# One gate product over two PSUM banks for a pair of channels, in a fused convolution block

## The chip, the cores and the metric

The kernel runs on one core of a Trainium2 chip. The metric is the device time of one execution in microseconds (us); the median of several executions is compared. PE is the matmul engine (PEld its weight loads, which overlap the matmuls), DVE the vector engine, ACT the scalar (activation) engine, POOL and SP issue DMAs. SBUF is the working memory, PSUM the memory in which matmuls add up, in eight banks of 512 fp32 values for each of 128 partitions.

## The reference

The input is 16 images of 192 channels and 64 x 64 pixels, in fp32. Two layers follow each other; the change lies in the first, between the two projections:

```python
h = layernorm_over_channels(x)
pg = conv1x1(h, in_proj_w, in_proj_b)             # 192 -> 384 channels
projected, gate = split(pg, 2, axis=1)
projected = dwconv3(projected, dw_k)              # 3x3, every channel by itself
scanned = directional_scan(projected, ...)        # s = d*s + (1-d)*cur, from left, right, top, bottom, mixed
local = dwconv3(projected, le_k)
mixed = (scanned + local) * sigmoid(gate)
bn = batchnorm(mixed)                             # mean and variance over images and pixels
x = x + conv1x1(gelu(bn), out_proj_w, out_proj_b)
x = x + fc2(gelu(fc1(layernorm_over_channels(x))))
```

The second layer multiplies every image with a 3 x 3 kernel of four taps that it computes from the image's means.

## The kernel before, in words

Three stages follow each other. The first (to about 640 us) normalizes, projects to 384 channels and writes the result to DRAM. The second (about 650 to 1326 us) does the convolutions, the scans, the gate and the statistics of the batch norm. The third (to the end) does everything else, per chunk of 512 pixels. The order of instructions on each engine is written out by hand: the instructions stand on every engine in the order in which the program issues them, and an engine waits at the head of its queue.

In the second stage the 192 channels are worked on in 24 groups of eight (GC = 8), and each group in four pairs (hp_ = 4) of channels c and c + 4, so that the loop runs over 96 pairs k. Partitions hold the columns of images (64 of one half of the 16 images, 64 of the other); a channel has 512 values per partition. The tile `pg` of a group holds all projected values (index 0) and gate values (index 1) of its eight channels, in 32 blocks of 16 values per channel, and there are three buffers of it (low, pg_o, mid). Per pair:

- `depthwise(k)` (L618): 40 matmuls over columns of `pg` into the PSUM tile `ps_d` (two banks, two buffers); ACT evacuates them to `q` (L631, L633).
- `tables(k)`, `scans(k)`: ACT writes two decay tables (L641), DVE runs a scan over all 1024 values forwards (L653) and one backwards (L655) into `v`.
- `local(k)` and `vertical(k)` (L662): 24 matmuls of `q` and then 16 of `v`, all adding into `ps_l`. Channel c adds into one bank and c + 4 into another. Each bank is a tile of its own, from four buffers.
- `sigmoid(k)` (L683): ACT writes the sigmoids of the two gate channels to two tiles `sg`, of which there are two buffers in all.
- `gate(k)`: for each of the two channels DVE multiplies the bank by the sigmoids (L696, 512 values) into the channel's place in `pg`, from which `bn_stats` (L697) takes the moments of that channel.

One round of the loop issues, in this order: tables of pair k+1; vertical and gate of pair k-1; scans of k+1; depthwise of k+2; local and sigmoid of k. So DVE's queue holds gate(k-1), scans(k+1), gate(k), and so on; PE's vertical(k-1), depthwise(k+2), local(k); ACT's tables(k+1), the evacuation of depthwise(k+2), sigmoid(k).

At the end of a group POOL stores its products to DRAM (L707), and SP loads the group three later into the same buffer (L605) once that store has landed. The matrices of the depthwise (dm, L190) and of the local and vertical matmuls (lm, L197) are loaded per group too, half on SP and half on POOL. `spread` and `batch_norm` turn the moments of the first 128 channels into scale and bias in rounds 76 and 77, with small matmuls (L723, L735) into tiles from the buffers of `ps_l`, and those of the last 64 after the loop; `hidden_bias` uses such a buffer before the loop. The third stage starts behind the last of these.

Of the kernel before, what the change touches and what calls it, by code (L numbers as in the profile page):

```python
# [21 lines left out]
F32 = mybir.dt.float32  # L22
# [9 lines left out]
CH = 512  # L32
# [8 lines left out]
GC = 8  # L41
NCG = C // GC
BR = 16
NB = HW // BR
# [11 lines left out]
def conv_block_kernel(ctx: ExitStack, tc: tile.TileContext, x, prm, w_in, w_out, w_fc1, b_fc1, w_fc2, w1, bn1, w2, out):  # L56
    nc = tc.nc
# [79 lines left out]
    def hidden_bias(pb):  # L137
        for m in range(NFC):
            for t in range(3):
                nc.tensor.matmul(pb[:, m:m + 1], wf1[0:64, t, 128 * m:128 * m + 128],  # L140
                                 pt3[0:64, t, LN2B:LN2B + 1], start=(t == 0), stop=(t == 2))
        nc.vector.tensor_add(bf1, bf1, pb[:, 0:NFC])
# [25 lines left out]
    stats = ce.tile([128, C, 6], F32, tag="stats", name="stats")  # L168
# [12 lines left out]
    lm_of = lambda g: lm_first if g == 1 else mats[g % 2]["lm"]  # L181
# [4 lines left out]
    def load_dm(g):  # L186
        for i, q in enumerate(HALF):
            v = dv_d[g, :, 0:1, :]
            src = bass.AP(v.tensor, v.offset, [[GC, HW], [128 * GC, 3], [1, HW * GC]])
            (nc.sync, nc.gpsimd)[i].dma_start(mats[g % 2]["dm"][q].rearrange("p k m c -> p k (m c)"), src)  # L190
# [396 lines left out]
    with ExitStack() as stage:  # L587
# [3 lines left out]
        wb = stage.enter_context(tc.tile_pool(name="wb", bufs=2))  # L591
        psb = stage.enter_context(tc.tile_pool(name="psb", bufs=2, space=PSUM))

        n_bp = C // 2
        hp_ = GC // 2
        grp = [dict() for _ in range(NCG)]
        bst = [dict() for _ in range(n_bp)]
# [38 lines left out]
        def tables(k):  # L636

            bst[k]["tab"] = []
            for d in range(2):
                tab = wb.tile([128, 2 * CH], F32, tag=f"tab{d}", name=f"tab{d}")  # L640
                nc.scalar.activation(tab.rearrange("p (n h) -> p n h", h=HW), mask[:, d].broadcast_to([128, n_img_all, HW]),  # L641
                                     AF.Copy, scale=dec_b[:, d, k:k + 1])
                bst[k]["tab"].append(tab)
# [14 lines left out]
        def lmul(k, m, src, dst, start, stop):  # L658
            g, c = divmod(k, hp_)
            for i, q in enumerate(HALF):  # L660
                for ih, o in enumerate(HALF):
                    nc.tensor.matmul(dst(bst[k]["ps"][i][o]), lm_of(g)[q, m, :, c], src(q, ih), start=start, stop=stop)  # L662

        def local(k):
            bst[k]["ps"] = [psb.tile([128, CH], F32, tag="l", name="ps_l", bufs=4) for _ in range(2)]
            img = lambda a: a.rearrange("p (n h) -> p n h", h=HW)
            q = bst[k]["q"]
            lmul(k, 1, lambda h, ih: q[h, ih], lambda a: a, True, False)
            lmul(k, 0, lambda h, ih: img(q[h, ih])[:, :, 0:HW - 1], lambda a: img(a)[:, :, 1:HW], False, False)
            lmul(k, 2, lambda h, ih: img(q[h, ih])[:, :, 1:HW], lambda a: img(a)[:, :, 0:HW - 1], False, False)  # L670

        def vertical(k):
            for d in range(2):
                lmul(k, 3 + d, lambda h, ih: bst[k]["v"][d][h, ih], lambda a: a, False, d == 1)

        def sigmoid(k):
            g, c = divmod(k, hp_)
            bst[k]["sg"] = []
            for i in range(2):
                ch = c + hp_ * i  # L680
                n = g * GC + ch
                sg = wb.tile([128, CH], F32, tag="sg", name="sg", bufs=2)
                nc.scalar.activation(sg.rearrange("p (i j b) -> p i j b", b=NB, j=BR),  # L683
                                     grp[g]["pg"][:, :, 1, ch].rearrange("p (i b) j -> p i j b", b=NB),
                                     AF.Sigmoid, bias=bias_g[:, n:n + 1])
                bst[k]["sg"].append(sg)

        def gate(k):
            g, c = divmod(k, hp_)
            s = grp[g]  # L690
            blocks = lambda a: a.rearrange("p (n j) -> p n j", j=BR)
            for i in range(2):
                ch = c + hp_ * i

                o = s["pg"][:, :, 0, ch]
                nc.vector.tensor_mul(o, blocks(bst[k]["ps"][i]), blocks(bst[k]["sg"][i]))  # L696
                nc.vector.bn_stats(stats[:, g * GC + ch], o)  # L697
            bst[k].clear()
            if c == hp_ - 1:
                if g == NCG - 1:  # L700

                    for i in range(2):
                        for wh in range(2):
                            w0_ = 32 * wh
                            (nc.sync, nc.gpsimd)[wh].dma_start(y_low[2 * w0_ + 32:2 * w0_ + 64, 2, i, LASTC * BR:],
                                                              s["pg"][w0_:w0_ + 32, i * NB, 0].rearrange("p c j -> p (c j)"))
                nc.gpsimd.dma_start(mixed_d[:, :, :, g].rearrange("i b p e -> p (i b) e"),  # L707
                                    s["pg"][:, :, 0].rearrange("p n c j -> p n (c j)"))
                s.clear()


        def moments(cls):
            chs = (slice(0, 128), slice(128, C))[cls]

            v = stats.rearrange("p c (e k) -> p k e c", k=3)
            return v[:, 1, :, chs], v[:, 2, :, chs], dev[:, :, chs]

        def spread(cls):
            means, sums2, dv = moments(cls)
            n = (128, C - 128)[cls]  # L720
            pm = psb.tile([128, CH], F32, tag="l", name="pm", bufs=4)
            for e in range(2):
                nc.tensor.matmul(pm[:, 0:n], ones, means[:, e], start=(e == 0), stop=(e == 1))  # L723
            nc.vector.scalar_tensor_tensor(dv, pm[:, 0:n].unsqueeze(1).broadcast_to([128, 2, n]), -1.0 / 256.0, means,
                                           ALU.mult, ALU.add)
            nc.vector.tensor_mul(dv, dv, dv)
            nc.vector.scalar_tensor_tensor(dv, sums2, 2.0 / (n_half * HW), dv, ALU.mult, ALU.add)

        def batch_norm(cls):
            means, _, dv = moments(cls)  # L730
            pq = psb.tile([128, CH], F32, tag="l", name="pq", bufs=4)
            for part in (slice(0, 128),) if cls == 0 else HALF:
                for j, src in enumerate((means, dv)):
                    for e in range(2):
                        nc.tensor.matmul(pq[part, j:j + 1], src[:, e], ones[:, 0:1], start=(e == 0), stop=(e == 1))  # L735
            nc.vector.tensor_scalar_mul(mv[:, cls], pq[:, 0:2], 1.0 / 256.0)
            sc, bi = bn_sc[:, cls:cls + 1], bn_bi[:, cls:cls + 1]
            nc.scalar.activation(sc, mv[:, cls, 1:2], AF.Sqrt, bias=eps5)
            nc.vector.reciprocal(sc, sc)
            nc.vector.tensor_mul(sc, sc, pv[:, cls, BNW:BNW + 1])  # L740
            nc.vector.tensor_mul(bi, sc, mv[:, cls, 0:1])
            nc.vector.tensor_sub(bi, pv[:, cls, BNB:BNB + 1], bi)
# [8 lines left out]
        for k in range(-2, n_bp + 1):  # L751
            if 0 <= k + 1 < n_bp:
                tables(k + 1)
            if k >= 1:
                vertical(k - 1)
                gate(k - 1)
                g, c = divmod(k, hp_)
                if c == 0 and 0 < g < NCG - 1:
                    load_lm(g + 1)
                if c == 0 and g == 3:  # L760
                    load_weights(2)
                if c == 0 and g + 2 < NCG:
                    load_pg(g + 2)
                if c == hp_ - 2 and g + 2 < NCG:
                    load_dm(g + 2)
            if 0 <= k + 1 < n_bp:
                scans(k + 1)
            if k == -2:
                hidden_bias(psb.tile([128, CH], F32, tag="l", name="pb_h", bufs=4))
            if k + 2 < n_bp:  # L770
                depthwise(k + 2)
            if 0 <= k < n_bp:
                local(k)
                sigmoid(k)
            if k in (1, 3, 5):
                scale_hidden(k // 2)
            if k == n_bp - 5 * hp_:
                spread(0)
            if k == n_bp - 5 * hp_ + 1:
                batch_norm(0)  # L780
            if k == n_bp - hp_:

                load_y(0, y_low, (nc.sync,), (0, 1))
                load_x2(0)
                load_x2(1)
            if k == n_bp - hp_ // 2:
                load_y(0, y_low, (nc.sync,), (2,), LASTC)
# [376 lines left out]
```

## Time and profile before

| | |
|---|---|
| median of 7 executions | 3753.4 us (3749.05 to 3757.9) |
| profiled execution | 3753.4 us, span 3751.6 us |
| busy in the span | PE 99%, PEld 44%, DVE 72%, ACT 48%, POOL 11% |
| DMA | 491.76 MB; 129 GB/s over the span, some 280 in the second stage |
| L696, products | 192 of 128x512, 0.67 us each |
| L697, bn_stats | 192 of 128x512, 0.69 us each |
| L653 and L655, scans | 96 each of 128x1024, 2.27 us each |
| L683, sigmoids | 192 of 128x512, 1.20 us each |

Times in the profile are counted from the start of the span. "Busy" for PE is modelled: matmuls are pipelined, and a PE that reads as 100% busy can still be waiting a little at each step. So the pace of a stage is better read from the starts of the same instruction in consecutive rounds than from busy time. An instruction's row may begin a little before the row ahead of it on its engine ends; what it costs its engine is the distance from start to start.

### The profile page before, as it was taken

The numbers are of one execution on the slowest core, as the hardware profiler recorded it, in microseconds if no ns is written. First come the engines' busy times: TensorE is split into PE (matmuls) and PEld (weight loads), VectorE is DVE, ScalarE is ACT, GpSimd is POOL, SyncE is SP. The second block draws the span as 40 slices with busy tenths as digits, with TensorE's granted clock in tenths as the row PEclk, the third lists the DMA queues.
The fourth block names the chain that finished last, engine by engine and source line by source line (L and its number), as shares of the span: only waits on it lengthen the run. The fifth ranks groups of instructions, "written<-read, shape, count | busy, mean of one in ns | idle before, by whom it ended". The sixth has DMA issues, their size and how long they took to land.

```text
span 3751.6 us, 71230 instructions
## 1 busy us (share of the span) xinstructions
PE 3697.6 (99%) x30252; PEld 1656.5 (44%) x30252; DVE 2716.5 (72%) x4260; ACT 1794.3 (48%) x1945; POOL 420.2 (11%) x683
## 2 busy tenths in 40 slices
PE   8999999999999979999999999999999999999998
PEld 5666666555555533333333333333333333333333
DVE  6887776999999965557756766666766775675763
ACT  3433444888888833334433434443443434443433
POOL 2334432101101020000000000000000000000000
PEclk9999999999999989999999999999999999999999
DMA  6899998999999950112222222222222221221212
GB/s 158 242 250 235 270 282 247 293 280 279 277 277 275 244 104 18 55 40 68 73 63 66 62 67 63 69 57 67 74 64 54 78 72 40 78 77 43 68 37 74
DMA packets 308429, 491.76 MB, mean 131 GB/s; under 512 B 46656, under 2 KB 202640, under 8 KB 308112
## 3 DMA queue, kind: packets, MB, share of 16 engines
q1 hardware_dynamic: 250064, 295.14, 29.6%
q0 software_dynamic: 57152, 190.94, 18.9%
q8 instruction: 239, 3.92, 0.4%
q10 hardware_dynamic: 896, 1.12, 0.1%
q14 instruction: 78, 0.64, 0.1%
HBM read 284.91 MB, written 197.92 MB: 129 GB/s over the span
## 4 chain that ended last, share of the span: by engine, by line
PE 95%; DVE 2%; DMA 1%; issue 1%; ACT 0%; SPq 0%; ACTq 0%; POOL 0%; DVEq 0%
PE ps_f L955 27%; PE ps_f L828 26%; PE ps_pj L512 13%; PE ps_l L662 10%; PE ps_d L618 6%; PE ps_o L887 5%; PE ps_xt L484 2%; PE ps_o L883 2%; PE ps_o L916 2%; DVE v L653 1%; DVE v L655 1%; DMA xa<-in_x_dram 1%; PE ps_k L828 0%; DMA out_dram<-ol 0%; DVE mid L696 0%
## 5 line engine op out<-in xcount | busy, mean ns | idle before, releaser
L957 ACT ACTIVATE gl<-ps_f,bf 128x1024 f32<-128x1024 f32 x384 | 427.6, 1114 | 1316.2 <-PE ps_f L955 1316.2
L955 PE MATMUL ps_f<-h,wf 64*64 64x512 f32 x9216 | 1035.9, 595 | 6.8 <-DVE h L943 6.7
L828 PE MATMUL ps_f<-gl,place 128*64 128x512 f32 x4608 | 1022.3, 592 | 0.0
L955 PEld LDWEIGHTS ps_f<-h,wf 64*64 64x64 f32 x9216 | 334.5, 133 | 693.8 <-issue 642.6
L828 PEld LDWEIGHTS ps_f<-gl,place 128*64 128x64 f32 x4608 | 334.2, 137 | 574.5 <-issue 533.4
L512 PE MATMUL ps_pj<-wi,xa 64*128 64x384 f32 x3072 | 515.7, 488 | 3.5 <-DVE stg L517 3.5
L923 DVE TENSOR_TENSOR h<-ximg,ps_o 128x768 f32<-128x768 f32 x128 | 116.4, 951 | 425.3 <-PE ps_o L887 417.0
L512 PEld LDWEIGHTS ps_pj<-wi,xa 64*128 64x128 f32 x3072 | 293.3, 188 | 198.0 <-issue 12.2
L893 DVE SCALAR_TENSOR_TENSOR ximg<-ps_o,pt,low 128x256 f32<-128x256 f32 x384 | 167.9, 479 | 267.4 <-PE ps_o L887 264.8
L65 DVE SCALAR_TENSOR_TENSOR o<-ximg,taps,o 128x1024 f32<-128x1024 f32 x252 | 323.1, 1282 | 8.7 <-ACT o L1014 2.6
L1018 POOL DMA_DIRECT2D out_dram<-o x168 | 87.9, 528 | 2067.6 <-DVE o L65 2064.8
L942 DVE RECIPROCAL rs<-rs 128x512 f32<-128x512 f32 x64 | 214.3, 3348 | 27.0 <-ACT rs L939 27.0
L653 DVE TENSOR_TENSOR_SCAN v<-tab,q 128x1024 f32<-128x1024 f32 x96 | 218.3, 2274 | 7.8 <-DMA pg_d<-mid 7.8
L655 DVE TENSOR_TENSOR_SCAN v<-tab,q 128x1024 f32<-128x1024 f32 x96 | 217.5, 2265 | 0.0
L518 ACT ACTIVATE stg<-ps_pj,rsa 128x384 f32<-128x384 f32 x128 | 119.8, 940 | 189.5 <-PE ps_pj L512 179.3
L887 PE MATMUL ps_o<-low,wo 128*64 128x256 f32 x1536 | 210.0, 395 | 0.0
L641 ACT ACTIVATE tab<-mask,dec_b 128x1024 f32<-128x1024 f32 x192 | 209.0, 1137 | 0.0
L518 ACT ACTIVATE mid<-ps_pj,rsa 128x384 f32<-128x384 f32 x128 | 120.5, 941 | 181.4 <-PE ps_pj L512 171.9
L491 DVE BATCH_NORM_STATS2 st<-ps_xt 128x6 f32<-128x192 f32 x512 | 173.0, 338 | 17.7 <-PE ps_xt L484 17.5
L239 DVE STREAM_TRANSPOSE low<-low 128x512 f32<-128x512 f32 x174 | 167.8, 1017 | 2.1 <-issue 0.3
L975 DVE SCALAR_TENSOR_TENSOR ximg<-ps_f,pt,ximg 128x512 f32<-128x512 f32 x192 | 134.4, 749 | 40.2 <-PE ps_f L828 37.8
L472 POOL DMA_DIRECT2D xa<-in_x_dram x192 | 119.8, 630 | 359.9 <-PE ps_pj L512 275.9
(197 smaller groups left out, 4105.9 us busy)
## 6 DMA issues: line engine op xcount, KB each, us to landing
low<-in_x_dram SPq DMA_DIRECT2D x128, 384.0 KB
out_dram<-o POOLq DMA_DIRECT2D x168, 256.0 KB, 3.7
mid<-pg_d SPq DMA_DIRECT2D x8, 4096.0 KB
low<-mixed_d SPq DMA_DIRECT2D x116, 256.0 KB
low<-pg_d SPq DMA_DIRECT2D x7, 4096.0 KB
pg_o<-pg_d SPq DMA_DIRECT2D x7, 4096.0 KB
xa<-in_x_dram POOLq DMA_DIRECT2D x192, 128.0 KB, 5.8
xa<-in_x_dram SPq DMA_DIRECT2D x192, 128.0 KB
```

The lines of the kernel that those rows point to most:

```text
L65: nc.vector.scalar_tensor_tensor(o, in0, scalar, in1, ALU.mult, ALU.add, **kw)
L512: nc.tensor.matmul(ps[i], pixels(n, t, g)[q], wi[q, t].rearrange("p g k c -> p (g k c)"), start=(t == 0), stop=(t == 2))
L518: nc.scalar.activation(stag[blk][1][:, :, j], ps[1], AF.Copy, scale=rs[:, g, 1:2])
L618: nc.tensor.matmul(dst(ps[o, ih]), mats[g % 2]["dm"][q, di + 1, :, ch], src(s["pg"][q, :, 0, ch]), start=(di == 0), stop=stop)
L653: nc.vector.tensor_tensor_scan(vf, tab, q, 0.0, ALU.mult, ALU.add)
L655: nc.vector.tensor_tensor_scan(vf[:, ::-1], tab[:, ::-1], q[:, ::-1], 0.0, ALU.mult, ALU.add)
L662: nc.tensor.matmul(dst(bst[k]["ps"][i][o]), lm_of(g)[q, m, :, c], src(q, ih), start=start, stop=stop)
L828: nc.tensor.matmul(ps[q], w(i), rhs(i), start=start, stop=stop)
L887: nc.tensor.matmul(ps[q, wh].rearrange("p (r w) -> p r w", w=32), wo[:, 64 * t:64 * t + 64], cols(rows(s["mx"][:, i]))[:, :, wh], start=Fa ...
L942: nc.vector.reciprocal(rs, rs)
L955: nc.tensor.matmul(pf[o, i], wf1[q, t, m0:m0 + 64], s["h"][q, t], start=(t == 0), stop=(t == 2))
L957: nc.scalar.activation(gl, pf, AF.Gelu, bias=bf1[:, m:m + 1])
```

## The change

The two banks of a pair become one PSUM tile of two banks (two buffers in place of four of one bank), and the two sigmoid tiles become one tile with one buffer; ACT still writes it with two instructions. One VectorE instruction then multiplies both banks by both sigmoids and writes the two channels' places in `pg`. The two `bn_stats` follow it. The small tiles of `spread`, `batch_norm` and `hidden_bias` take the first bank of such a two-bank tile.

```diff
-                    nc.tensor.matmul(dst(bst[k]["ps"][i][o]), lm_of(g)[q, m, :, c], src(q, ih), start=start, stop=stop)
+                    nc.tensor.matmul(dst(bst[k]["ps"][o, i]), lm_of(g)[q, m, :, c], src(q, ih), start=start, stop=stop)
...
-            bst[k]["ps"] = [psb.tile([128, CH], F32, tag="l", name="ps_l", bufs=4) for _ in range(2)]
+            bst[k]["ps"] = psb.tile([128, 2, CH], F32, tag="l", name="ps_l")
...
-            bst[k]["sg"] = []
+            bst[k]["sg"] = wb.tile([128, 2, CH], F32, tag="sg", name="sg", bufs=1)
             for i in range(2):
                 ch = c + hp_ * i
                 n = g * GC + ch
-                sg = wb.tile([128, CH], F32, tag="sg", name="sg", bufs=2)
-                nc.scalar.activation(sg.rearrange("p (i j b) -> p i j b", b=NB, j=BR),
+                nc.scalar.activation(bst[k]["sg"][:, i].rearrange("p (i j b) -> p i j b", b=NB, j=BR),
                                      grp[g]["pg"][:, :, 1, ch].rearrange("p (i b) j -> p i j b", b=NB),
                                      AF.Sigmoid, bias=bias_g[:, n:n + 1])
-                bst[k]["sg"].append(sg)
...
-            blocks = lambda a: a.rearrange("p (n j) -> p n j", j=BR)
+            blocks = lambda a: a.rearrange("p i (n j) -> p i n j", j=BR)
+
+            o = s["pg"][:, :, 0, c::hp_].rearrange("p n i j -> p i n j")
+            nc.vector.tensor_mul(o, blocks(bst[k]["ps"]), blocks(bst[k]["sg"]))
             for i in range(2):
-                ch = c + hp_ * i
-
-                o = s["pg"][:, :, 0, ch]
-                nc.vector.tensor_mul(o, blocks(bst[k]["ps"][i]), blocks(bst[k]["sg"][i]))
-                nc.vector.bn_stats(stats[:, g * GC + ch], o)
+                nc.vector.bn_stats(stats[:, g * GC + c + hp_ * i], o[:, i])
...
-            pm = psb.tile([128, CH], F32, tag="l", name="pm", bufs=4)
+            pm = psb.tile([128, 2, CH], F32, tag="l", name="pm")[:, 0]
...
-            pq = psb.tile([128, CH], F32, tag="l", name="pq", bufs=4)
+            pq = psb.tile([128, 2, CH], F32, tag="l", name="pq")[:, 0]
...
-                hidden_bias(psb.tile([128, CH], F32, tag="l", name="pb_h", bufs=4))
+                hidden_bias(psb.tile([128, 2, CH], F32, tag="l", name="pb_h")[:, 0])
```

## The prediction

> **What bounds the kernel now.** The profiled execution took 3753.4 us, span 3751.6, and 3753.4 is also the median of the seven runs, so sums made in its times stand against the median as they are. The change lies in the second stage (the loop over 96 channel pairs, about 650 to 1326 us). I read first the busy times in stretches of that stage (columns: us, PE, PEld, DVE, ACT, POOL busy, granted clock, DMA share, GB/s):
>
> ```profile
> 653.00:895.00 242.00, 242.00 (x2820) 130.67 (x2816) 239.68 (x207) 212.21 (x253) 25.26 (x25) 1.00 1.03 285
> 900.00:1100.00 200.00, 200.00 (x2300) 108.48 (x2296) 198.09 (x171) 170.01 (x201) 21.53 (x21) 1.00 1.05 277
> ```
>
> PE, DVE and DMA all read as full, so busy time does not say which one sets the pace. The chain of waits, by its starts, does:
>
> ```profile
> 867.02 4.28 PE ps_l L662 x40
> 873.91 4.28 PE ps_l L662 x40
> ...
> 1048.55 4.39 PE ps_l L662 x40
> 1055.56 4.39 PE ps_l L662 x40
> ```
>
> Up to about 895 us PE starts a pair every 6.89 us (4.28 of L662, 2.61 of L618: no gap). Later it takes 7.00. The list of waits says why: its weight loads wait for the second scan of a pair (us in total, times, longest; 700 to 1300 us), while the other waits for DVE in that list, 0.2 us each, leave PE no gap.
>
> ```profile
> PEld ps_l L662 <- DVE v L655: 23.7, 45, 0.7
> ```
>
> One pair on DVE, in order of time:
>
> ```profile
> 904.64 0.66 DVE L696 TENSOR_TENSOR mid<-ps_l,sg 128x512 f32<-128x512 f32 x1
> 905.34 0.69 DVE L697 BATCH_NORM_STATS2 stats<-mid 128x6 f32<-128x512 f32 x1
> 905.95 0.67 DVE L696 TENSOR_TENSOR mid<-ps_l,sg 128x512 f32<-128x512 f32 x1
> 906.65 0.69 DVE L697 BATCH_NORM_STATS2 stats<-mid 128x6 f32<-128x512 f32 x1
> 907.26 2.27 DVE L653 TENSOR_TENSOR_SCAN v<-tab,q 128x1024 f32<-128x1024 f32 x1
> 909.45 2.26 DVE L655 TENSOR_TENSOR_SCAN v<-tab,q 128x1024 f32<-128x1024 f32 x1
> 911.64 0.66 DVE L696 TENSOR_TENSOR low<-ps_l,sg 128x512 f32<-128x512 f32 x1
> ```
>
> From start to start: 0.70 + 0.61 + 0.70 + 0.61 + 2.19 + 2.19 = 7.00 us, without a gap. A product holds DVE 0.70 (the bn_stats behind it reads what it wrote), a bn_stats only 0.61 of its 0.69 (the next instruction does not need its result). So DVE is the bound of the whole stage: from the first scan at 650.85 to the end of the last bn_stats (1325.20 + 0.69 = 1325.9) are 675.05 us, and 96 x 7.00 plus the batch-norm instructions in between (1.64 and 1.15 us) are 674.8. Up to 895 PE merely ran ahead on its buffers, 0.11 us a pair. What follows the stage begins with a matmul that waits for that last bn_stats, so its end moves everything behind it.
>
> **The change part by part.** *Products.* 192 products of 512 elements become 96 of 1024. A product has 0.533 us for 512 elements at the slope of these rows (L923: 768 elements in 951 ns, L943: 1536 in 1758, 1.05 ns each) and 0.137 beside it (0.67); the other TENSOR_TENSOR rows have 0.151 to 0.159 beside their slope.
>
> ```profile
> L923 DVE TENSOR_TENSOR h<-ximg,ps_o 128x768 f32<-128x768 f32 x128 | 116.4, 951 | 425.3 <-PE ps_o L887 417.0 <-PE ps_o L916 8.3
> L943 DVE TENSOR_TENSOR h<-h,rs 128x1536 f32<-128x1536 f32 x64 | 112.5, 1758 | 2.2
> L65 DVE SCALAR_TENSOR_TENSOR o<-ximg,taps,o 128x1024 f32<-128x1024 f32 x252 | 323.1, 1282 | 8.7 <-ACT o L1014 2.6
> ```
>
> The wide one: 1.067 + 0.137 = 1.20 us, and 1.24 to the bn_stats behind it with the 0.03 seen now. L923 has a three-level output and a PSUM input, as the wide product has. No DVE row here reads two PSUM banks in one instruction. On ACT, L957 does (1024 elements, 1114 ns) and is no slower than L641 from SBUF (1137). Bounds: 1.10 below (slope and 0.03 alone), 1.31 above (L65, the slowest plain row of 1024 elements, plus 0.03); I take 1.24, since the operation is L923's and L696's own.
>
> *bn_stats.* Both stay, 0.61 each; the second no longer has a product ahead of it. DVE's pair is 1.24 + 0.61 + 0.61 + 4.38 = 6.84 us against 7.00: one fixed cost of 0.16 is saved, 96 times, 15.4 us.
>
> *Where it stops.* 6.84 is below PE's 6.89, so PE takes over. Its second-stage work begins with L662 of pair 0 at 653.39: 93 rounds of 6.89, three last pairs without a depthwise of 4.28 each, and 1.16 + 1.43 for the batch-norm matmuls after channel 128: 653.39 + 640.8 + 12.8 + 2.6 = 1309.6. DVE alone would be through at 1310.5 (1325.9 - 15.4). Pair 0's product starts 1.9 us after its matmuls end (659.60 against 655.78 + 1.89), and DVE gains 0.05 a pair on PE, so from about pair 38 on the product waits for PE. Near the end: L662 of pair 93 ends 2 x 4.28 before 1309.6, at 1301.0; products of pair 93 at 1301.1, of pair 94 one DVE pair later at 1307.9.
>
> *Sigmoids in one tile.* Both sigmoids of pair k+1 now wait for the wide product of pair k (1.24 after its start, before 0.70 for the first). In the loop this is covered: the two sigmoids take 2.3 us, the product that needs them comes 6.84 after the last one; behind them on ACT's queue stand the tables (2.1) and the depthwise evacuation (1.5), 5.9 us of work in 6.89, and scans and PE need those a pair later. The cover is gone only at the last pair, which has no scans ahead of it: sigmoids from 1309.15 to 1311.5, so the last product starts at 1311.5 instead of 1310.3: 1.1 us lost. End of the stage: 1311.5 + 1.24 + 0.61 + 0.69 = 1314.0, against 1325.9: **11.9 us less**. Here the Trainium skill speaks against the change: Perfetto Trace Analysis, section "Optimizing Scalar/DVE Operations", says that larger instructions help a saturated engine, while one that makes others wait may be done sooner in pieces. By the first half the fixed part on PSUM is estimated at 125 ns, 12 us over 96 pairs; the second half is true of that last pair alone.
>
> *PSUM slots.* Two slots of two banks instead of four banks. The first L662 of pair k+2 waits for the product of pair k in either case: now for its first product at 905.30 and second at 906.62, PE being there at 908.4; the wide one ends at 905.9. Cost nothing, covered by the depthwise of 2.61 in between. The batch-norm matmuls take a whole slot; the pair behind waits for a DVE instruction that ends some 3 us before PE asks. Nothing.
>
> *Queues.* No DMA is added or moved. POOL's store of a group (L707) waits for the last product of it and SP's load of the group three later (L605) for that store; both come earlier with DVE.
>
> Sum: 3753.4 - 11.9 = 3741.5 us.
>
> **The rivals.** *A: the wide product keeps part of what it should save.* If the second bank costs what an independent instruction does (bn_stats: 0.61 - 0.533 = 0.077 saved instead of 0.16), DVE's pair is 6.92 and DVE stays the bound: 96 x 0.077 - 1.1 = 6.3 us, 3747.1. With L65's 1.31 it is 96 x 0.09 - 1.1 = 7.5, 3745.9. Against: the two products' pitch is 0.70, not 0.61, and each removed one takes all of it. The Trainium skill (Vector Engine (DVE) Microarchitecture Reference, section "Measured stream behaviour on trn2") gives 75 ns per instruction, an estimated 7.2 us less the tail; the bn_stats pitch agrees, that of the products doesn't. Chance 0.11.
>
> *B: DMA becomes the bound.* Its share reads 1.03 to 1.06 throughout and PE lost 0.85 us at 1109.81, at the first depthwise of a group, with ACT's sigmoid named, which its wait is not on. If a group's transfers can't be done in less than the present 28.0 us, PE (27.56 a group) loses 0.44 in each of the 15 groups after the first nine, 6.6 us, less a margin of 0 to 3 that the loads have now: gain 12 - 6.6 to 12 - 3.6, 3745 to 3748. Against: stores start when the last product of a group ends, and these come earlier, for DVE no longer lags 5.7 us behind PE (904.64 against the end of PE's own part at 898.92). Chance 0.10.
>
> *C: slower.* The wide product itself costs more than the two it replaces: by the place where banks and channels change (output rows jump from channel c to c + 4, PSUM crosses a bank) it would have to stand over 1.39 us to the next bn_stats to give back the gain with the tail, and every 0.01 above costs 0.96 us: at 1.50, 96 x 0.10 + 1.1 = 10.7 us, 3764. For it: no DVE row shows the crossing. Against: L957 crosses banks at no price, L923 walks three levels at none. Chance 0.09 slower by over 0.2%, 0.05 for a stall that just eats the gain (3751).
>
> **How the numbers follow.** Forecast (gain 10 to 13 us, 3740 to 3744): 0.65; A 0.11; B 0.10; no change 0.05; C 0.09. The predicted time is the likeliest case's, 3741.5. Its own range is 3738 to 3745 (PE's limit and 1.10 below, where the product is never late; a wide product of 1.27 above; 2 us of the scatter of medians). To leave out no more than 2 in 10, the range has to take in A and B: 3738 to 3750. About 0.2%, 7.5 us, is what a measurement of this kernel can tell from no change. Of A and B about a third falls below 3745.9: faster 0.73, same 0.17, slower 0.10.
>
> **What would show it.** L696 should have 96 rows of 128x1024, 1.20 to 1.22 us each; from start to start of L653 less than 7.00; PE's pairs 6.89 apart throughout, the wait for v of L655 gone from PEld's list, and in its place DVE idle ahead of L696, released by ps_l, from about pair 38; the sigmoids waiting on L696 to its end; third-stage rows unchanged in length and some 12 us earlier. Wrong: rows of 1.3 us or more (A, C), or idle time of PE at the first depthwise of groups (B).

## The result, and the profile after

The changed kernel takes 3743.5 us (median of 15 runs, 3738.2 to 3748.5) against 3753.3 us for the kernel before, run beside it (35 runs, 3748.7 to 3761.4). The ratio is 0.9974, with a 95% interval from 0.9967 to 0.9980: 9.7 us less, by the interval 7.5 to 12.4. Forecast were 3741.5 us, with a range of 3738 to 3750. The second stage, counted as the forecast counts it from pair 0's first scan to the end of the last bn_stats, went from 675.05 to 663.64 us: 11.4 us less, a little under the 11.9 of the forecast. In the changed kernel the product stands in L692, bn_stats in L694 and the sigmoids in L682.

First, the busy times in the two stretches that were shown of before, now of the changed kernel (us, then PE, PEld, DVE, ACT and POOL busy, granted clock, DMA share, GB/s):

```profile
653.00:895.00 242.00, 242.00 (x2812) 137.87 (x2808) 239.95 (x177) 210.47 (x254) 25.29 (x25) 1.00 1.04 299
900.00:1100.00 200.00, 200.00 (x2328) 114.49 (x2324) 199.00 (x146) 169.46 (x203) 23.73 (x23) 1.00 1.06 282
```

PE, DVE and DMA read as full as they did before, so this view tells as little as then. What changed is the pace, in the chain of waits (start, us, engine, operation and line):

```profile
872.90 4.28 PE ps_l L662 x40
879.78 4.28 PE ps_l L662 x40
...
1045.19 4.28 PE ps_l L662 x40
1052.08 4.28 PE ps_l L662 x40
```

PE starts a pair every 6.89 us in both stretches; before, the second read 7.00. The reason is in the waits of PE's weight loads (700 to 1280 us; us in total, times, longest):

```profile
PEld ps_l L662 <- DVE v L653: 1.7, 8, 0.2
PEld ps_l L662 <- DVE stats L694: 0.8, 4, 0.2
PEld ps_d L618 <- ACT tab L641: 0.2, 1, 0.2
```

The waits for the second scan, v of L655, are gone (before, 23.5 us in 44 of them in this window). What is left are the entries above, 2.7 us in all, two waits of 0.7 us at the matmuls of the batch norm, and entries named issue, of 0.4 us at most, in which the engine waits for nothing that the profile shows.

The product's rows by tile (shortest, median and longest ns; first and last start):

```profile
L692 DVE TENSOR_TENSOR low<-ps_l,sg x32: 1195/1224/1226, 659.6 to 1259.5; 128x1024 f32<-128x1024 f32 x32
L692 DVE TENSOR_TENSOR pg_o<-ps_l,sg x32: 1196/1220/1225, 686.8 to 1286.9; 128x1024 f32<-128x1024 f32 x32
L692 DVE TENSOR_TENSOR mid<-ps_l,sg x32: 1194/1223/1225, 714.1 to 1311.0; 128x1024 f32<-128x1024 f32 x32
```

All 96 lie between 1.194 and 1.226 us: an access across two PSUM banks, with an output that jumps over channels, costs no more than its elements and one fixed part. The group of low is the first, that of pg_o the second: its first product comes 27.2 us later, four pairs of 6.81.

The first product of all starts late:

```profile
659.56 1.22 DVE L692 TENSOR_TENSOR low<-ps_l,sg 128x1024 f32<-128x1024 f32 x1 [0.85 <-ACT sg L682]
```

It needs both sigmoids of its pair, where the narrow one needed the first alone. From the first scan (649.87) to this product it is 9.69 us; before it was 8.75 (650.85 to 659.60). The end of the stage does not feel this, since DVE makes it up: it keeps its own 6.81 us a pair until it has caught up with PE, as the starts of the products show (rows between them left out):

```profile
877.47 1.20 DVE L692 TENSOR_TENSOR mid<-ps_l,sg 128x1024 f32<-128x1024 f32 x1
...
884.28 1.20 DVE L692 TENSOR_TENSOR mid<-ps_l,sg 128x1024 f32<-128x1024 f32 x1
...
891.10 1.22 DVE L692 TENSOR_TENSOR mid<-ps_l,sg 128x1024 f32<-128x1024 f32 x1
...
898.01 1.23 DVE L692 TENSOR_TENSOR mid<-ps_l,sg 128x1024 f32<-128x1024 f32 x1
```

The product at 891.10 is that of pair 34. From there to the batch-norm rounds (about 1175 us) the products start 6.85 to 6.92 us apart; behind those rounds it is 6.81 again for eleven pairs, until DVE has caught up once more.

Then a pair in the middle of the stage, on DVE in order of time (start, duration):

```profile
904.86 1.23 DVE L692 TENSOR_TENSOR low<-ps_l,sg 128x1024 f32<-128x1024 f32 x1
906.12 1.29 DVE L694 BATCH_NORM_STATS2 stats<-low 128x6 f32<-128x512 f32 x2
907.33 2.27 DVE L653 TENSOR_TENSOR_SCAN v<-tab,q 128x1024 f32<-128x1024 f32 x1
909.52 2.27 DVE L655 TENSOR_TENSOR_SCAN v<-tab,q 128x1024 f32<-128x1024 f32 x1
911.77 1.22 DVE L692 TENSOR_TENSOR low<-ps_l,sg 128x1024 f32<-128x1024 f32 x1
```

From product to product it is 6.91 us here, near PE's pace and not DVE's own 6.81. Most of the difference stands between the second scan and the product, 2.25 us instead of the 2.18 that it takes where nothing is waited for. The view gives no idle time there; the gap is too short for it.

The end of the stage, on DVE and on ACT:

```profile
1307.49 1.20 DVE L692 TENSOR_TENSOR mid<-ps_l,sg 128x1024 f32<-128x1024 f32 x1
1308.72 1.29 DVE L694 BATCH_NORM_STATS2 stats<-mid 128x6 f32<-128x512 f32 x2
1310.97 1.23 DVE L692 TENSOR_TENSOR mid<-ps_l,sg 128x1024 f32<-128x1024 f32 x1 [0.96 <-ACT sg L682]
1312.23 1.29 DVE L694 BATCH_NORM_STATS2 stats<-mid 128x6 f32<-128x512 f32 x2
```

```profile
1308.72 2.21 ACT L682 ACTIVATE sg<-mid,bias_g 128x512 f32<-128x512 f32 x2 [4.30 <-DVE mid L692]
```

The last two sigmoids wait for the wide product of pair 94 to end, and the last product waits for them, 0.96 us. The last bn_stats ends at 1313.5, against 1325.9 before; 1.0 us of that is the first scan, which came earlier in this execution (649.87 against 650.85) in a stage that the change doesn't touch.

The first matmul of the third stage, before and then after:

```profile
1363.16 7.92 PE L955 MATMUL ps_f<-h,wf 64*64 64x512 f32 x48 [6.71 <-DVE h L943]
```

```profile
1350.91 7.94 PE L952 MATMUL ps_f<-h,wf 64*64 64x512 f32 x48 [6.71 <-DVE h L940]
```

It comes 12.25 us earlier behind the same wait of 6.71, and PE's last matmul still is 12.3 us earlier (it ends at 3731.9 instead of 3744.2). The span is only 10.6 us shorter: 1.0 by the earlier first scan and 11.4 by the second stage, less 1.8 behind it, since what follows PE's last matmul took 9.1 us instead of 7.4. There an eviction into ol waits for the store of the one before it:

```profile
3735.03 1.11 ACT L1037 ACTIVATE ol<-ps_d,pt 128x1024 f32<-128x1024 f32 x1 [4.34 <-DMA out_dram<-ol]
```

Whether the change lengthens that wait was asked in a run of its own (the fifth below).

### The profile page after: what moved, and what is told of

It reads as the page before. It is cut to its first block, busy times and chain, and to the rows that moved or that the text cites. A ratio compares the mean times of both kernels' runs of the same rounds, so it can differ in the third digit from the quotient of the medians.

```text
span 3741.0 us, 71017 instructions
## 1 busy us (share of the span) xinstructions
PE 3687.9 (99%) x30252; PEld 1665.2 (45%) x30252; DVE 2705.2 (72%) x4164; ACT 1785.4 (48%) x1945; POOL 420.2 (11%) x683
## 4 chain that ended last, share of the span: by engine, by line
PE 96%; DMA 2%; DVE 1%; SPq 0%; POOL 0%; ACT 0%; issue 0%; ACTq 0%; POOLq 0%
PE ps_f L952 27%; PE ps_f L825 26%; PE ps_pj L512 13%; PE ps_l L662 11%; PE ps_d L618 7%; PE ps_o L884 5%; PE ps_xt L484 2%; PE ps_o L880 2%; PE ps_o L913 1%; DMA xa<-in_x_dram 1%; PE ps_k L825 0%; DMA mixed_d<-mid 0%; DMA ximg<-mixed_d 0%; DMA out_dram<-ol 0%; PE ps_d L1035 0%; DVE ol L65 0%
## 5 line engine op out<-in xcount | busy, mean ns | idle before, releaser
L653 DVE TENSOR_TENSOR_SCAN v<-tab,q 128x1024 f32<-128x1024 f32 x96 | 218.3, 2274 | 7.0 <-ACT tab L641 7.0
L655 DVE TENSOR_TENSOR_SCAN v<-tab,q 128x1024 f32<-128x1024 f32 x96 | 217.5, 2265 | 0.0
```

Source lines behind the costliest of these rows:

```text
L653: nc.vector.tensor_tensor_scan(vf, tab, q, 0.0, ALU.mult, ALU.add)
L655: nc.vector.tensor_tensor_scan(vf[:, ::-1], tab[:, ::-1], q[:, ::-1], 0.0, ALU.mult, ALU.add)
```

## The experiments

The first four ran on a second chip, where the kernel before takes 3761.1 us (23 runs); the last three on a third, where it takes 3758.0 us (22 runs). Ratios are to these. "Stage" is, in every case, the time from pair 0's first scan to the end of the last product or bn_stats in the profiled execution: 675.05 us before, 663.64 us after. The fifth expectation counts from pair 0's product instead, which gives 666.29 and 653.96 us, 12.3 less; that count flatters a wide product by 0.9 us, since it leaves out the wait at the first pair. Where a kernel has lines added, its line numbers have moved on by one to three: L655 in the last two runs is the first scan, L653 of before.

### The tiles alone, with two products

```diff
-            o = s["pg"][:, :, 0, c::hp_].rearrange("p n i j -> p i n j")
-            nc.vector.tensor_mul(o, blocks(bst[k]["ps"]), blocks(bst[k]["sg"]))
             for i in range(2):
-                nc.vector.bn_stats(stats[:, g * GC + c + hp_ * i], o[:, i])
+                o = s["pg"][:, :, 0, c + hp_ * i]
+                nc.vector.tensor_mul(o, blocks(bst[k]["ps"][:, i]), blocks(bst[k]["sg"][:, i]))
+                nc.vector.bn_stats(stats[:, g * GC + c + hp_ * i], o)
```

(against the changed kernel; blocks is that of before)

> The changed tiles (one PSUM tile of two banks, one sigmoid tile), but two products of 512 elements again. Theory (the gain is the one fixed cost of 0.16 us a pair on DVE): DVE's pair is back at 7.00 us, the scans stand 7.00 apart, the stage ends near 1325.9, time 3753 us, within 0.2% of before. Rival (part of the gain or of what was lost of it comes from the tiles: fewer slots and waits, one buffer of sigmoids): 3748 us or less, or over 3761.

Measured: 3760.4 us, ratio 1.0000 (0.9991 to 1.0009), stage 675.64 us. DVE in order of time:

```profile
1000.00 0.67 DVE L694 TENSOR_TENSOR low<-ps_l,sg 128x512 f32<-128x512 f32 x1
...
1001.32 2.27 DVE L653 TENSOR_TENSOR_SCAN v<-tab,q 128x1024 f32<-128x1024 f32 x1
...
1008.32 2.27 DVE L653 TENSOR_TENSOR_SCAN v<-tab,q 128x1024 f32<-128x1024 f32 x1
```

and among the waits of PE's weight loads (700 to 1280 us):

```profile
PEld ps_l L662 <- DVE v L655: 25.1, 48, 0.6
```

DVE's pair is 7.00 us again, and PE waits for the second scan again. The two-bank PSUM slots and the single tile for the sigmoids neither give nor take anything in the loop; all of the gain comes from the one instruction. The stage is 0.6 us longer than before, and that lies at the last pair: its first product waits 0.50 us for its sigmoids and starts 3.21 us after that of the pair ahead, 2.63 before.

### The last pair's sigmoids into another buffer

```diff
-            bst[k]["sg"] = wb.tile([128, 2, CH], F32, tag="sg", name="sg", bufs=1)
+            if k == n_bp - 1:
+                bst[k]["sg"] = wb.tile([128, 2, CH], F32, tag="q", name="sg_q", bufs=3)
+            else:
+                bst[k]["sg"] = wb.tile([128, 2, CH], F32, tag="sg", name="sg", bufs=1)
```

> The changed kernel, but the sigmoids of the last pair go to a free buffer of q, so that they need not wait for the product of the pair before. Theory (the tail's 1 us is the wait of the last product for its sigmoids, 0.96 us in the trace): that wait is gone, the last bn_stats ends 1.0 us earlier, 3742.5 us beside the changed kernel's 3743.5; all earlier pairs as they were. Rival (the chain of waits of the changed kernel goes from the last product through a store and a load to the third stage, so the transfers set its start): the last bn_stats is earlier, the first L952 of the third stage is not.

Measured: 3748.6 us, ratio 0.9965 (0.9954 to 0.9977), stage 662.67 us, 0.97 less than with the change alone. The end of the stage on DVE:

```profile
1317.26 1.20 DVE L695 TENSOR_TENSOR mid<-ps_l,sg 128x1024 f32<-128x1024 f32 x1
1318.50 1.29 DVE L697 BATCH_NORM_STATS2 stats<-mid 128x6 f32<-128x512 f32 x2
1319.70 1.21 DVE L695 TENSOR_TENSOR mid<-ps_l,sg_q 128x1024 f32<-128x1024 f32 x1
```

The last product follows at once, so the wait of 0.96 us was what the single tile costs at the last pair. The rival fell too: from the first scan to the first matmul of the third stage it is 700.31 us instead of 701.04, so 0.7 us arrive there. This is the best version by the stage among those that compute everything; that it beats the change end to end can't be told from 1 us in medians with intervals of this width (0.9965 here, 0.9974 and 0.9968 for the change).

### One bn_stats a pair, in the changed kernel

```diff
-            for i in range(2):
+            for i in range(1):
                 nc.vector.bn_stats(stats[:, g * GC + c + hp_ * i], o[:, i])
```

(in this run and the next, stats is also filled with ones once, ahead of the loop)

> The changed kernel without the bn_stats of the second channel of each pair, so the batch norm of those 96 channels is left out; DVE has 0.61 us less in each pair. Theory (PE is the bound of the loop now, 6.89 us a pair): PE's pairs stay 6.89 apart, DVE stands idle some 0.6 us more a pair ahead of the product; only the last two pairs, where DVE is alone, bring 1.2 us: 3742 us. Rival (DVE still sets the pace): 96 x 0.61 = 58 us less, 3685.

Measured: 3748.9 us, ratio 0.9965 (0.9954 to 0.9976), stage 662.50 us. DVE is relieved by 0.61 us a pair, 58.6 us over 96 pairs, and 1.1 us of it come through, half of that the bn_stats that is missing at the very end. DVE's waits (700 to 1280 us) and one of them in order of time:

```profile
DVE mid L693 <- PE ps_l L663: 12.0, 21, 0.6
DVE low L693 <- PE ps_l L663: 11.6, 21, 0.6
DVE pg_o L693 <- PE ps_l L663: 10.5, 19, 0.6
```

```profile
902.57 1.22 DVE L693 TENSOR_TENSOR mid<-ps_l,sg 128x1024 f32<-128x1024 f32 x1 [0.56 <-PE ps_l L663]
```

The product waits for PE's matmuls in 61 pairs of that stretch, and in 20 others for the sigmoids; PE's own rounds stay 6.89 us apart. So in the changed kernel PE is the bound, and DVE has nothing more to give.

### One bn_stats a pair, in the kernel before

```diff
-                nc.vector.bn_stats(stats[:, g * GC + ch], o)
+                if i == 0:
+                    nc.vector.bn_stats(stats[:, g * GC + ch], o)
```

> The kernel before without the bn_stats of the second channel of each pair (the batch norm of those 96 channels is left out): DVE's pair is 6.39 us, with narrow products, four banks and two sigmoid tiles. Theory (any relief of DVE is worth what PE lets through): PE's pairs 6.89 apart throughout, the last bn_stats or product near 1311.7 instead of 1325.9, 14 us less, 3739 us, although 58 us were taken off DVE. Rival (the wide product helps by something else than DVE's time): this one stays near 3753, or goes below 3725 because PE could do better than 6.89.

Measured: 3748.1 us, ratio 0.9964 (0.9951 to 0.9977); stage 661.27 us to the end of the last product, which here comes after the last bn_stats (660.68): 13.8 to 14.4 less than before. The chain of waits, and DVE in order of time:

```profile
906.88 4.28 PE ps_l L663 x40
913.77 4.28 PE ps_l L663 x40
```

```profile
1000.85 0.69 DVE L697 TENSOR_TENSOR low<-ps_l,sg 128x512 f32<-128x512 f32 x1 [0.51 <-PE ps_l L663]
1001.57 0.69 DVE L699 BATCH_NORM_STATS2 stats<-low 128x6 f32<-128x512 f32 x1
1002.18 0.67 DVE L697 TENSOR_TENSOR low<-ps_l,sg 128x512 f32<-128x512 f32 x1
1002.77 2.28 DVE L654 TENSOR_TENSOR_SCAN v<-tab,q 128x1024 f32<-128x1024 f32 x1
```

Quite another relief of DVE, with no part of the change and almost four times as much a pair (0.61 for the bn_stats and 0.11 for the product that it followed, 0.72 instead of 7.00 - 6.81 = 0.19), buys the same 6.89: PE's matmuls on v for the last pair start 657.27 us after the first scan here and 657.28 in the changed kernel. The stage is 2.4 us shorter than with the change, all of it behind that point, at the last pair. The gain in the loop is what DVE's pair was above PE's, not how much work DVE loses. The 0.11 is read from the rows: the second product, which no bn_stats reads here, holds DVE 0.59 us to the next instruction, where one with its bn_stats behind it holds it 0.70 in the kernel before (here the first product has waited, and holds it 0.72).

### The changed kernel once more

On a third chip, with no edit.

> The changed kernel once more, unchanged. In its first trace the second stage, from pair 0's product to the end of the last bn_stats, is 12.3 us shorter than before, while the median was only 9.7 us lower. Theory (the 2.6 us between them are scatter of the first stage and of the last transfers): the stage is 654 us long again, and the ratio lies nearer to the trace's 12.3 us, 0.9966 to 0.9975. Rival (something behind the stage gives 2.6 us back each time): from the last bn_stats to the end of the span it is longer than the 2425.7 us of before by 2 to 3 us again.

Measured: 3744.5 us, ratio 0.9968 (0.9956 to 0.9980), 13.5 us less than the kernel before; stage 663.70 us, or 654.01 from the first product; ratio and stage are as the theory expected. The eviction near the end, which waited 4.34 us in the first profile of this same kernel:

```profile
3732.52 1.11 ACT L1037 ACTIVATE ol<-ps_d,pt 128x1024 f32<-128x1024 f32 x1 [2.61 <-DMA out_dram<-ol]
```

From the end of the last bn_stats to the end of the span it is 2425.4 us here, 2425.7 in the kernel before (on the first chip), and 2425.6 and 2425.0 in the two runs below, which were traced on the same chip. So nothing of the gain is given back behind the stage here, and the rival fell on this chip. Elsewhere it stays open: the same stretch took 2427.5 us in the first profile, and on the second chip 2428.3 to 2428.8 in the three kernels with a shorter stage against 2426.3 in that with two products; on the first chip nearly all of the difference lies behind PE's last matmul (9.1 us against 7.4), on the second a part of it (9.1 against 8.4). One trace of each can't tell whether the kernel, the chip or the execution does this. The medians of the second chip show no such loss: 12.5, 12.2 and 13.0 us less than before, where the stage has 12.4, 12.5 and 13.8.

The two medians for the change, 9.7 and 13.5 us, have intervals of 7.5 to 12.4 and 7.5 to 16.5 us, and the 11.4 of the stage lie in both, so the difference between them needs no cause. The first scan alone comes between 649.4 and 659.6 us in the nine traces, in a stage that the change doesn't touch.

### DVE made slower again, by 64 and by 128 elements

```diff
             for i in range(2):
                 nc.vector.bn_stats(stats[:, g * GC + c + hp_ * i], o[:, i])
+            nc.vector.tensor_mul(pad, ones[:, 0:64], ones[:, 0:64])
```

(the lines that make the tile pad and fill it once are left out)

> The changed kernel with one more DVE instruction behind the bn_stats of every pair, a product of 64 constant elements into a tile that nobody reads. By the bn_stats pitch (0.077 beside the slope) it costs 0.14 us: DVE's pair goes from the 6.81 of the trace to 6.95. Theory (DVE is the bound again as soon as its pair is over PE's 6.89): 96 x 0.05 - 1.1 = 3.7 us faster than before, against 12 without it, ratio 0.999. Rival (what counts is that there is one product and one wait less, or the two-bank tiles): still about 12 us faster, 0.9968.

Measured: 3753.6 us, ratio 0.9989 (0.9980 to 0.9998), stage 671.44 us, 3.6 less than before. DVE in order of time, and the wait of PE's weight loads for the second scan (700 to 1280 us), which is back:

```profile
1047.49 2.28 DVE L655 TENSOR_TENSOR_SCAN v<-tab,q 128x1024 f32<-128x1024 f32 x1
...
1054.31 0.21 DVE L697 TENSOR_TENSOR pad<-ones 128x64 f32<-128x64 f32 x1
1054.44 2.28 DVE L655 TENSOR_TENSOR_SCAN v<-tab,q 128x1024 f32<-128x1024 f32 x1
```

```profile
PEld ps_l L664 <- DVE v L657: 17.4, 33, 0.6
```

The same edit with 128 elements:

> The same with 128 constant elements, 0.21 us: DVE's pair is 7.02 us. Theory: 96 x 0.02 + 1.1 = 3 us slower than before, ratio 1.0008; between this one and the one with 64 elements lie 96 x 0.067 = 6.4 us. Rival (as there): still about 12 us faster.

Measured: 3757.2 us, ratio 1.0000 (0.9991 to 1.0009), stage 677.69 us, 2.6 more than before. The medians can't confirm the 3 us of the expectation: they show 0.8 us less, with an interval of some 3.4 us to either side. The same two views:

```profile
1050.75 0.27 DVE L697 TENSOR_TENSOR pad<-ones 128x128 f32<-128x128 f32 x1
1050.94 2.28 DVE L655 TENSOR_TENSOR_SCAN v<-tab,q 128x1024 f32<-128x1024 f32 x1
...
1057.95 2.28 DVE L655 TENSOR_TENSOR_SCAN v<-tab,q 128x1024 f32<-128x1024 f32 x1
```

```profile
PEld ps_l L664 <- DVE v L657: 35.2, 56, 0.7
```

The small instruction holds DVE 0.13 and 0.19 us, and the pair takes 6.95 and 7.01 us (6.81 + 0.13 would be 6.94, and 6.81 + 0.19 is 7.00). Put side by side with the other kernels, the stage follows DVE's own pair only where that is above PE's 6.89:

| kernel | DVE's own pair, us | stage, us |
|---|---|---|
| one bn_stats, changed | 6.81 - 0.61 = 6.20 | 662.50 |
| changed | 6.81 | 663.64 |
| changed, 64 elements more | 6.95 | 671.44 |
| before | 7.00 | 675.05 |
| changed, 128 elements more | 7.01 | 677.69 |

From 6.20 to 6.81 the stage moves by 1.1 us. From 6.95 to 7.01 it moves by 6.3, about the 5.6 that 0.06 makes in the 94 gaps between products that have scans in them (a difference of two rounded numbers, so good to 0.01 a pair, or 0.9 us). The row of before has narrow products, which wait at neither end of the loop; the wide ones of the last row lose 0.85 us at the first pair and 0.77 at the last, so the 2.6 us between these two rows are more than the 0.01 a pair makes.

## Why the prediction was right

- **DVE as the bound, 7.00 us a pair.** Right. It rested on starts and on the waits of the weight loads, not on busy time. The kernel before with less for DVE to do falls to PE's 6.89, and the changed one with 128 elements more goes back to 7.01 and to the time of before.
- **The wide product at 1.20 us, 1.24 to the next instruction.** Right: 1.20 where it comes without a wait, and 1.24 (1317.26 to 1318.50). Both bounds, 1.10 and 1.31, were further off than the value taken from L923 and L696. One reading in it is off: by the slope of L923 and L943, 807 ns for 768 elements or 1.051 each, 512 elements are 0.538 us and not 0.533. The fixed part of a product is then 0.132, that of those two rows 0.144, and that of a bn_stats 0.072; no term of the sum moves by more than 0.01. DVE's pair came out 0.03 shorter than the forecast's 6.84: 1.24 + 1.20 for both bn_stats + 2.19 + 2.18 = 6.81.
- **Where it stops: PE takes over at 6.89.** Right, and the term that kept the forecast from 15.4 us. PE's part of the stage ends at 1309.06 (1309.6 forecast), but it began 1.0 us earlier than the forecast's 653.39, so it took 0.5 longer than forecast. Most of this is the batch norm: its three rounds, from 1171.61 to 1195.26, take 23.65 us instead of 3 x 6.89, 3.0 more where the forecast put 2.6. The run with one bn_stats in the changed kernel shows that PE is then the bound.
- **The sigmoids, 1.1 us at the last pair and nothing in the loop.** Right at the last pair: 0.96 us, and the run with another buffer for it takes just that away. That the cover is gone only there was not right: the product also waits for its sigmoids at the first pair, 0.85 us, and at 1198.18, behind the batch-norm rounds, 0.76 us. Neither reaches the end of the stage, since PE's rounds go on at 6.89 and DVE catches up with them. The Trainium skill (Perfetto Trace Analysis, section "Optimizing Scalar/DVE Operations") has both halves of this: grouping can help a saturated engine, and where the engine isn't saturated but makes others wait, smaller pieces may be done sooner. The runs agree with each: the loop, where DVE was the bound, gained by the one wide product, and at the last pair the product waits 0.96 us where it is wide and 0.50 where it is two.
- **PSUM slots and queues at nothing.** Right: the tiles alone with two products leave 675.6 us of stage against 675.1, and the 0.6 between them are the sigmoids of the last pair.
- **The sum.** The stage gave 11.4 us against 11.9, and the batch-norm rounds are most of the difference. The medians gave 9.7 and 13.5 on two chips, a scatter to which the forecast gave 2 us: 2.2 below its 11.9 and 1.6 above. The shares of the cases do not quite give the chances of its last line: 0.65 and a third of 0.21 are 0.72 for faster, the rest of the 0.21 and the 0.05 are 0.19 for the same, and 0.09 is left for slower.
- **The rivals.** A (part of the gain kept by the second bank) and C (a wide product above 1.39 us) fell with the first 96 rows, none above 1.226. B (DMA as the bound) fell with the chain of waits: PE's first 75 gaps from round to round are all 6.89 or 6.90, through the changes of group, while DMA moves 299 and 282 GB/s in the two stretches instead of 285 and 277, so the transfers had some room left.
- **One sign was misjudged.** "DVE idle ahead of L692, released by ps_l, from about pair 38" isn't among the waits of the changed kernel. The wait is there from pair 34 on, but at some 0.08 us a pair (6.89 - 6.81) it shows only as a later start (2.25 instead of 2.18) and as a product row of 1.22 instead of 1.20. With DVE relieved further, it is listed, 0.56 us in the row shown. That 34 came so near 38 is partly luck: DVE gained 0.08 a pair and not 0.05, but it began 2.9 us behind PE's first pair and not 1.9 (659.56 against 656.65), as the first product waited for its sigmoids.

## What to carry to other kernels

When several engines read as fully busy, compare starts: the pace of each engine's rounds, and the pace that it keeps when it waits for nothing, tell which one is the bound and what the next one allows. Relief of the bound is worth the difference to the next engine's pace and no more, here 0.11 of the 0.19 us saved a pair (0.72 and 0.80 us a pair bought the same 6.89, and 2.4 and 1.1 us more at the end of the loop), so work out the second pace before costing the first. Where two small tiles become a large one, look at the first and the last round of the loop, which have no other work to cover the longer wait: both waited here, and only the last one cost time.

## What the runs showed of the hardware

- The fixed cost of a DVE instruction depends on who comes next. A product of 512 elements takes 0.70 us to the start of a bn_stats that reads it, and 0.59 us to the start of a scan that doesn't; at 1.05 ns an element that is 0.16 and 0.05 us beside the elements. The small products of 64 and 128 elements, whose result nobody reads, take 0.13 and 0.19 us: 0.06 beside theirs. The Trainium skill (Vector Engine (DVE) Microarchitecture Reference, section "Measured stream behaviour on trn2") gives 75 ns for each instruction: near the cost without a reader, half of that with one, so here the rows decide. Joining two instructions saved the larger of these costs here, as each product had its reader right behind it.
- The followers above differ in kind too, a bn_stats or a scan. Among the products behind the batch norm's matmuls, of one element a partition, the follower is a product in both cases: L738, whose result L739 reads, holds DVE 0.20 us; L739, whose result L692 doesn't read, 0.08.

```profile
1190.23 0.16 DVE L738 TENSOR_TENSOR bn_bi<-bn_sc,mv 128x1 f32<-128x1 f32 x1
1190.43 0.16 DVE L739 TENSOR_TENSOR bn_bi<-pv,bn_bi 128x1 f32<-128x1 f32 x1
1190.51 1.22 DVE L692 TENSOR_TENSOR pg_o<-ps_l,sg 128x1024 f32<-128x1024 f32 x1
```

- Reading two PSUM banks in one DVE instruction costs nothing that the rows show: 1.194 to 1.226 us for 1024 elements, against 1.076 by the slope plus the 0.132 that one product of a single bank has beside it, 1.21.
